# Attention in quarter steps with a written TensorE order, and experts gated sequence by sequence, in a two-layer kernel

## The chip, the core and the metric

The kernel runs on one core of a Trainium2 chip. It has five engines that run side by side and wait for each other through semaphores: TensorE (PE; its weight loads are shown as PEld), VectorE (DVE), ScalarE (ACT), GpSimd (POOL) and SyncE (SP), which here only starts transfers. The metric is the device time of one execution in microseconds. All data are float32.

## What is computed

Eight sequences of 256 tokens with 256 features pass four blocks, each added to its input after a layer norm:

```python
x = x + attn(layernorm(x))     # w = x @ W.T in 16 heads of 16; q, k, v = rms_norm(w) * g1, g2, g3
                               # att = q k^T / 4; score = softmax(att, -1) + softmax(att, -2)
                               # (score @ v) @ W
x = x + moe(layernorm(x))      # 4 experts, 2 for each token, silu(x w1) * (x w3) @ w2,
                               # and one shared expert for all tokens
x = x + rwkv(layernorm(x))     # time mixing: three recurrences along the tokens of a sequence
x = x + moe2(layernorm(x))     # 8 experts with biases, 2 for each token,
                               # g * sigmoid(1.702 g) * (l + 1) @ w2
```

Queries and keys come from the same w, so the att matrix of one head is symmetric. Exponentials computed once therefore serve both softmaxes, which have the same sums.

## The kernel before

The kernel writes its instructions as a Python program over tiles. A scheduler then puts each engine's instructions in an order of its own, by their place in the program and by estimated times, and adds the waits. Tiles come from pools; a pool holds so many buffers of each name, and a new tile waits until a buffer of that name is free. PSUM has three kinds of buffers here: `sc` for scores, `ps` for transposes, projections and values, `mm` for the experts' products.

The sequences are handled in two groups: five (`GROUPS[0]`) and three (`GROUPS[1]`). The experts of each block take their tokens group by group. A group passes these parts, methods of the class `Experts`: `front` (layer norm, transposes and gate for each sequence, then the choice of two experts and `route`, which works out a slot for each token), `sends` (POOL scatters tokens to DRAM, two transfers for each 128 tokens), `shared` (the expert for all tokens, or in the second layer the biases), `tiles` (128 sorted tokens at a time: fetch, transpose, up, transpose, down, write back) and `combine` (POOL gathers the results, DVE adds them). In `tiles` the stages of neighbouring tiles overlap: a step fetches tile j+3, transposes j+1, does up for j, transposes the hidden values of j-1 and does down for j-2. In the second layer the product that makes `h` stands on POOL (line 807).

Attention is `attention_bounded` (from line 404). For each sequence, `prepare` does the norm, transposes, projection (line 433) and the rms norm of all heads at once: squares on ACT, sums on DVE, the power -1/2 on POOL (line 442), and the product `n` on DVE (line 444). `turn` transposes `n` (line 453) and makes keys, queries and values. For each half of the heads (`u`) and each half of the tokens (`t`), `exponentials` does four score matmuls of 32 rows by 512 columns (line 477), their exponentials on ACT (lines 482 and 490), and sums, reciprocals and scaled values `nv` on DVE. `values` multiplies them (line 505), for one parity of heads at a time over both token halves; `project_heads` transposes the result, adds its two parts, transposes again and projects (line 536). The generator `steps` walks through this: while the exponentials of one half are made, the values of the half before are multiplied.

`layers` puts the parts together. `weave` takes several generators, each with a number, and advances the one that is behind its share, so their instructions stand in the program in turn; `take` cuts a generator. Group one's attention stands alone, with four `ps` and four `sc` buffers. Then come two `ps`, three `sc` and three `mm`, and the parts of the experts are woven with the attention of group two:

```python
weave((one.front(), 7), (take(attention, 3), 3))
weave((one.sends(), 10), (one.shared(), 5), (take(attention, 8), 8))
tiles = one.tiles()
weave((take(tiles, 12), 12), (attention, 16))
actx.close()
weave((two.front(), 5), (take(tiles, 3), 3))
weave((two.sends(), 6), (tiles, 10))
```

The second layer is built in the same way, with time mixing (`rwkv`, a generator of some eight steps for each sequence, of which two run at once) in attention's place: the first group's mixing is woven with the tiles of group two, and the second group's with the second layer's experts.

Of the kernel before, what the change touches and what calls it, by code (L numbers as in the profile page):

```python
# [13 lines left out]
AX = mybir.AxisListType  # L14

P = 128
B, T, D = 8, 256, 256
NTOK = B * T
NC = D // P
# [47 lines left out]
def two_layers(  # L67
# [336 lines left out]
    def attention_bounded(ap1, ap2, ep, fresh):  # L404
# [21 lines left out]
        def prepare(b):  # L426

            ps = fresh()[0]
            xt = turned(layer_norm(ap2, b, "xn"), ap2, "xnT", ps, nc.scalar)
            pw = ps([P, TT, D])  # L430
# [12 lines left out]
            n = ap2.tile([P, TT, NH, DH], F32, tag="n", name="n", bufs=3)  # L443
            nc.vector.tensor_tensor(n, pw4, rr.unsqueeze(3).to_broadcast([P, TT, NH, DH]), ALU.mult)
            seq[b] = dict(n=n)
# [55 lines left out]
        def values(b, u, es, par, py):  # L501

            for t in range(TT):
                for p in range(4):
                    nc.tensor.matmul(
                        py[STRIP * p : STRIP * (p + 1), par, :],
                        lhsT=seq[b]["nv"][:, t, 8 * u + 2 * p + par, :],
                        rhs=es[t, p][:, par, :],
                        start=(t == 0),
                        stop=(t == TT - 1),  # L510
                    )
            if par:
                nc.scalar.copy(seq[b]["yT"][:, u], py)

        def project_heads(b):
            ps = fresh()[0]
            q = seq.pop(b)
            y = ap2.tile([P, TT, NH, DH], F32, tag="y", name="y")
            for t in range(TT):
                pz = ps([P, 2, 4, 2, 2 * DH])  # L520
                for u in range(2):
                    for par in range(2):
                        nc.tensor.transpose(pz[:, u, :, par, :], q["yT"][:, u, par, ts(t, P)], ident)
                z = pz.rearrange("p u k a d -> p (u k a) d")
                nc.vector.tensor_tensor(
                    y[:, t],
                    z[:, :, DH:],
                    q["r"][:, t, :].unsqueeze(2).to_broadcast([P, NH, DH]),
                    ALU.mult,
                )  # L530
                nc.vector.tensor_tensor(y[:, t], y[:, t], z[:, :, 0:DH], ALU.add)
            yT = turned(y.rearrange("p t h d -> p t (h d)"), ap2, "yT2", ps, nc.scalar)
            po = ps([P, TT, D])
# [7 lines left out]
        def steps(seqs):  # L541

            prepare(seqs[0])
            yield
            turn(seqs[0])
            yield
            before = None
            for b, after in zip(seqs, seqs[1:] + (None,)):
                for u in range(2):
                    es = {}  # L550
                    py = fresh()[0]([P, 2, T]) if before else None
                    for t in range(TT):
                        exponentials(b, u, t, es)
                        if before:
                            values(*before, t, py)
                        yield
                    if before and before[1]:
                        project_heads(before[0])
                    yield
                    if after is not None:  # L560
                        (turn if u else prepare)(after)
                    yield
                    before = (b, u, es)
            py = fresh()[0]([P, 2, T])
            for par in range(2):
                values(*before, par, py)
            project_heads(before[0])
            yield

        return steps  # L570

# [22 lines left out]
    class Experts:  # L594
# [7 lines left out]
        def __init__(self, layer, k, weights, lnp, mp, rt, ps, mm):  # L602
# [5 lines left out]
            self.sent, self.back = (d[k][0 : P * self.n_tiles, :] for d in (sent, back))  # L608

        def front(self):  # L610

            rt, ps, nt, n = self.rt, self.ps, self.nt, self.n_experts
            self.xns, self.xts = [], []
            gw = (gw1, gw2)[self.layer]
            logit = rt.tile([P, nt, n], F32, tag="logit", name="logit")
            for i, b in enumerate(self.seqs):
                xn = layer_norm(self.lnp, b, "xm", bufs=max(len(g) for g in GROUPS))
                xt = turned(xn, self.mp, "xmT", ps, nc.scalar, bufs=2 if self.layer else max(len(g) for g in GROUPS))
                self.xns.append(xn)
                self.xts.append(xt)  # L620
                lg = ps([P, TT, n])
                for t in range(TT):
                    for c in range(NC):
                        nc.tensor.matmul(
                            lg[:, t, :], lhsT=xt[:, c, ts(t, P)], rhs=gw[:, c, :], start=(c == 0), stop=(c == NC - 1)
                        )
                to = logit[:, TT * i : TT * (i + 1), :]
                if self.layer:
                    nc.vector.tensor_tensor(to, lg, gb2.unsqueeze(1).to_broadcast([P, TT, n]), ALU.add)
                else:  # L630
                    nc.vector.tensor_copy(to, lg)
                yield
# [404 lines left out]
    def layers(is_bounded):  # L1037
# [4 lines left out]
        with ExitStack() as pctx, ExitStack() as ctx0, ExitStack() as actx:  # L1042
# [14 lines left out]
            if is_bounded:  # L1057
# [3 lines left out]
                with ExitStack() as p1:  # L1061
# [3 lines left out]
                    for _ in steps(GROUPS[0]):  # L1065
                        pass
# [121 lines left out]
```

## Time and profile before

| | us |
|---|---|
| median of three runs | 982.57 (981.32 to 987.0) |
| the profiled execution, as a run | 987.99 |
| its span, first to last instruction | 986.2 |
| attention of the first five: first score to last output projection | 34.3 to 209.7 |
| gates of those five; logits of the last | 210.4 to 235.9 |
| sends of the first group | 250.6 to 282.0 |
| tiles of the first group | 294.2 to 486.4 |
| sends of the first group in the second layer | 717.0 to 743.6 |
| last product of the tiles | 960.8 |

Times of stages are read from the trace, in microseconds from the first instruction. Several of the parts run at once; the table only gives their ends. A matmul in float32 leaves two records. The profile's granted clock is the share of full speed that TensorE's throttle allows; over the span it is 0.867. POOL's power of 128x32 (line 442) takes 5433 ns on average, eight times in all; each send and gather (lines 715 and 844) about 996 ns, 64 times each. A table load on ACT takes 1283 ns.

### The profile page before, as it was taken

The page shows a single profiled execution, that of the slowest core. Times are in us where ns is not written, and L with a number is a line of the kernel's source. Part 1 is how long each engine was busy: PE and PEld are TensorE (multiplying, and loading weights), DVE is VectorE, ACT ScalarE, POOL GpSimd, SP SyncE. Part 2 cuts the span into 40 slices and gives each one's busy share as a digit, 9 for nine tenths or more (in the row PEclk, how much of TensorE's full clock was granted, in tenths as well). Part 3 has the DMA queues.
Part 4 walks back from the last instruction along what each step waited for, and adds up shares of the span by engine and source line. Part 5 has one row for each costly group of instructions (what it writes and reads, how often), then busy time and mean ns, then how long its engine had stood idle before and what let it go on. Part 6 is the DMA issues. An engine that isn't in the chain of part 4 may idle for free. (4 is left out here: it accounts for less than half of the span.)

```text
span 986.2 us, 11005 instructions
## 1 busy us (share of the span) xinstructions
PE 786.5 (80%) x3248; PEld 466.8 (47%) x3248; DVE 497.8 (50%) x1173; ACT 362.2 (37%) x697; POOL 278.0 (28%) x357
## 2 busy tenths in 40 slices
PE   2787987988699899999969989855376988596890
PEld 1323423355455445665746665544243655353550
DVE  4453453524334333331256888887856784334432
ACT  1342442424347556542215525531213363222330
POOL 4313112002731100012171112234173232516424
PEclk9967767757899999999989999996657999799995
DMA  8820000000120001122130000014821211224413
GB/s 265 297 80 1 1 0 1 1 0 1 59 71 21 29 20 36 59 68 90 52 99 27 27 27 17 17 32 132 259 86 64 70 59 50 90 65 143 134 61 104
DMA packets 57763, 66.98 MB, mean 68 GB/s; under 512 B 7480, under 2 KB 51552, under 8 KB 57696
## 3 DMA queue, kind: packets, MB, share of 16 engines
q1 hardware_dynamic: 50016, 48.79, 15.4%
q0 software_dynamic: 6144, 16.79, 5.4%
q10 hardware_dynamic: 1536, 0.60, 0.2%
q8 instruction: 31, 0.51, 0.2%
q14 instruction: 36, 0.29, 0.1%
HBM read 38.61 MB, written 27.54 MB: 67 GB/s over the span
## 5 line engine op out<-in xcount | busy, mean ns | idle before, releaser
L477 PE MATMUL sc<-qT,kT 32*128 32x512 f32 x256 | 112.6, 791 | 4.3 <-ACT e L490 4.3
L176 POOL TENSOR_TENSOR rs<-mv,eps_ln 128x2 f32<-128x2 f32 x32 | 7.2, 228 | 329.5 <-DVE mv L174 279.8
L791 PE MATMUL mm<-v1s,xgT 128*128 x184 | 92.0, 623 | 0.0
L785 ACT COPY hT<-ps 128x256 f32<-128x256 f32 (+1 forms) x84 | 39.3, 468 | 136.7 <-PE ps L783 128.1
L715 POOL DMA_INDIRECT sent<-xm,slot x64 | 63.7, 996 | 83.3 <-DVE pick L690 65.3
L490 ACT ACTIVATE e<-sc,minus 128x512 f32<-128x512 f32 x96 | 62.4, 693 | 65.9 <-PE sc L477 43.6
L491 DVE TENSOR_REDUCE s<-e 128x2 f32<-128x512 f32 x96 | 62.6, 681 | 42.5 <-ACT e L490 42.0
L844 POOL DMA_INDIRECT y<-back,slot x64 | 63.7, 995 | 69.4 <-DMA back<-yg 41.6
L791 PE MATMUL mm<-w3s,xgT 128*128 x152 | 73.0, 597 | 3.1 <-DVE h L813 3.1
L791 PE MATMUL mm<-w1s,xgT 128*128 x152 | 74.3, 608 | 1.4 <-issue 1.4
L791 PE MATMUL mm<-w2s,hT 128*128 x304 | 72.2, 379 | 0.0
L783 PEld LDWEIGHTS ps<-ident,h 128*128 128x128 f32 x244 | 30.8, 143 | 66.7 <-issue 34.1
L807 POOL TENSOR_TENSOR h<-h,hb 128x256 f32<-128x256 f32 x46 | 34.7, 756 | 94.3 <-ACT h L806 94.2
L783 PE MATMUL ps<-ident,h 128*128 128x128 f32 x244 | 42.7, 281 | 21.4 <-POOL h L807 15.3
L791 PEld LDWEIGHTS mm<-w2s,hT 128*128 128x128 f32 x304 | 54.7, 190 | 6.3 <-issue 0.5
L818 DVE COPY yg<-mm 128x256 f32<-128x256 f32 x84 | 35.4, 421 | 44.0 <-PE mm L791 39.0
L813 DVE TENSOR_TENSOR h<-h,mm 128x512 f32<-128x512 f32 x38 | 25.9, 681 | 57.6 <-PE mm L791 44.9
L804 DVE TENSOR_TENSOR hb<-mm,b1rows 128x512 f32<-128x512 f32 x46 | 31.6, 687 | 43.6 <-PE mm L791 34.7
L442 POOL TENSOR_TENSOR rr<-rr,minus_half 128x32 f32<-128x32 f32 x8 | 43.5, 5433 | 31.5 <-DVE rr L441 31.5
L847 DVE SCALAR_TENSOR_TENSOR x<-y,share,x 128x256 f32<-128x256 f32 x64 | 31.6, 499 | 40.7 <-DMA y<-back,slot 39.5
L785 ACT COPY xgT<-ps 128x256 f32<-128x256 f32 x84 | 31.0, 370 | 57.5 <-PE ps L783 44.1
L791 PE MATMUL mm<-v2s,hT 128*128 x184 | 50.7, 400 | 0.8 <-ACT hT L785 0.8
(209 smaller groups left out, 1413.3 us busy)
## 6 DMA issues: line engine op xcount, KB each, us to landing
xg<-sent SPq DMA_DIRECT2D x84, 128.0 KB
back<-yg SPq DMA_DIRECT2D x84, 128.0 KB
sent<-zero SPq DMA_DIRECT2D x46, 128.0 KB
x<-in_x_dram SPq DMA_DIRECT2D x8, 256.0 KB
w1s<-in_w_dram SPq DMA_DIRECT2D x4, 512.0 KB
w3s<-in_w_dram SPq DMA_DIRECT2D x4, 512.0 KB
w2s<-in_w_dram SPq DMA_DIRECT2D x4, 512.0 KB
v1s<-in_v1g_dram SPq DMA_DIRECT2D x8, 256.0 KB
```

The costliest lines, as they stand in the source:

```text
L442: nc.gpsimd.tensor_tensor(rr, rr, minus_half.rearrange("p (t h) -> p t h", h=NH), ALU.pow)
L477: nc.tensor.matmul(pa, lhsT=q["kT"][rows, u, ts(t, P)], rhs=q["qT"][rows, u], start=True, stop=True)
L490: nc.scalar.activation(e, pa, AF.Exp, bias=minus)
L491: nc.vector.tensor_reduce(q["s"][:, t, h : h + 2], e, AX.X, ALU.add)
L715: inst = nc.gpsimd.indirect_dma_start(out=self.sent, out_offset=self.index(k, t), in_=self.xns[t // TT][:, t % TT, :], in_offset=None).ins
L783: nc.tensor.transpose(pt[:, c, :], src[:, ts(c, P)], ident)
L785: nc.scalar.copy(to, pt)
L791: nc.tensor.matmul(po.unsqueeze(1), lhsT=lhsT[:, c, :], rhs=w[:, ds(e, 1), c, :], start=(c == 0), stop=(c == n - 1))
L804: nc.vector.tensor_tensor(hb.unsqueeze(1), ph.unsqueeze(1), self.weights[2][:, ds(e_dve, 1), :], ALU.add)
L807: nc.gpsimd.tensor_tensor(s, s, hb[:, I2:], ALU.mult)
L818: nc.vector.tensor_copy(yg, py)
L844: nc.gpsimd.indirect_dma_start(out=y, out_offset=None, in_=self.back, in_offset=self.index(k, at))
```

## The change

Attention's stages become separate functions: `norm`, `project_in`, `turn`, `exponentials`, `values`, `to_tokens`, `turn_back`, `project_heads`. The new `steps` gives each of them a step number for each sequence, four steps to a sequence, and emits within a step in a fixed order of functions. `values` now does one token half and both parities, a step after its exponentials. The gate of layer one (`norm`, `flip`, `judge`) follows each sequence in the same steps. Around attention, `tc.manual_schedule(engines={ENG.PE})` keeps TensorE's instructions in the order in which the program has them; the other engines keep the scheduler's. `front` is cut: its part for one sequence is `norm`, `flip` and `judge`; the rest is `choose`. Time mixing calls a function at each sequence's end, which does the gate of layer two. Buffers change: `e` 10 to 9, `n` 3 to 2; in the stage of attention with experts `mm` 3 to 2 and `ps` 2 to 3. In the second layer, for its last group of experts (`self.last`), the product for `h` is on DVE.

```diff
-        def values(b, u, es, par, py):
+        def values(b, u, t, es):
-            for t in range(TT):
+            q = seq[b]
+            if t == 0:
+                q["py"] = fresh()[0]([P, 2, T])
+            for par in range(2):
                 for p in range(4):
...
-                        start=(t == 0),
-                        stop=(t == TT - 1),
+                        start=(t == 0 and par == 0),
+                        stop=(t == TT - 1 and par == 1),
                     )
-            if par:
-                nc.scalar.copy(seq[b]["yT"][:, u], py)
+            if t == TT - 1:
+                nc.scalar.copy(q["yT"][:, u], q["py"])
...
+        def steps(seqs, after):
+            late = {}
+            def at(n, f, *args):
+                late.setdefault(n, []).append((f, args))
+            for i, b in enumerate(seqs):
+                n = 4 * i + 4
+                at(max(n - 5, 0), norm, b)
+                at(max(n - 4, 0), project_in, b)
+                at(n - 2, turn, b)
                 for u in range(2):
                     es = {}
                     for t in range(TT):
+                        at(n + 2 * u + t, exponentials, b, u, t, es)
+                        at(n + 2 * u + t + 1, values, b, u, t, es)
+                    at(n + 2 * u + 3, to_tokens, b, u)
+                at(n + 6, turn_back, b)
+                at(n + 7, project_heads, b)
+                for k, f in enumerate(after):
+                    at(n + 7 + k, f, b)
+            order = (norm, turn, exponentials, project_in, to_tokens, values, turn_back, project_heads) + tuple(after)
+            for n in range(max(late) + 1):
+                for f, args in sorted(late.get(n, []), key=lambda x: order.index(x[0])):
+                    f(*args)
+                yield
...
-                    nc.gpsimd.tensor_tensor(s, s, hb[:, I2:], ALU.mult)
+                    (nc.vector if self.last else nc.gpsimd).tensor_tensor(s, s, hb[:, I2:], ALU.mult)
...
+                    with tc.manual_schedule(engines={ENG.PE}):
+                        for _ in steps(GROUPS[0], (one.norm, one.flip, one.judge)):
+                            pass
...
+                psum.update(pool=p2.enter_context(tc.tile_pool(name="p2", bufs=1, space=PSUM)), mm=2, ps=3, sc=3)
+                one.choose()
+                tiles = one.tiles()
+                if is_bounded:
+                    attention = steps(GROUPS[1], (two.norm, two.flip, two.judge))
+                    with tc.manual_schedule(engines={ENG.PE}):
+                        weave((one.sends(), 10), (take(attention, 6), 6), (one.shared(), 5))
+                        weave((take(tiles, 12), 12), (attention, 13))
+                    actx.close()
...
+            two.choose()
+            weave((two.sends(), 6), (tiles, 13))
...
-            weave((mixing(GROUPS[0]), 36), (tiles, 15))
+            weave((mixing(GROUPS[0], norm_of(three)), 36), (tiles, 15))
+            three.choose()
             weave((two.combine(), 3))
...
+            ahead = mixing(GROUPS[1], norm_of(four))
+            weave((three.sends(), 10), (three.shared(), 5), (take(ahead, 6), 6))
+            tiles = three.tiles()
+            weave((take(tiles, 17), 17), (ahead, 16))
+            four.choose()
+            weave((take(tiles, 3), 3))
+            weave((four.sends(), 6), (four.shared(), 3), (tiles, 9))
+            weave((three.combine(), 5), (four.tiles(), 21))
+            weave((four.combine(), 3))
```

`one` and `two` are the groups of layer one; `three` and `four` those of layer two, which were also called `one` and `two` before.

## The prediction

> **What bounds the kernel now.** I read four views in this order: the page's slices, the busy time by stage, the timeline of one sequence of the first attention stage, and the list of waits. The page says that no engine is full over the span, and that the TensorE clock is short in slices 2 to 11.
>
> ```profile
> PE 786.5 (80%) x3248; PEld 466.8 (47%) x3248; DVE 497.8 (50%) x1173; ACT 362.2 (37%) x697; POOL 278.0 (28%) x357
> PEclk9967767757899999999989999996657999799995
> ```
>
> The stages: five sequences of attention alone (34 to 210 us), attention of three sequences beside expert tiles (294 to 405), tiles (to 486), then time mixing beside tiles, the second layer's experts, and the last tiles.
>
> ```profile
> 115.50:153.00 37.50, 31.73 (x134) 13.15 (x133) 16.52 (x40) 14.46 (x34) 7.98 (x7) 0.73 0.00 1
> 352.00:405.60 53.60, 52.36 (x248) 27.67 (x242) 19.90 (x43) 35.89 (x60) 0.89 (x2) 1.00 0.10 30
> 580.00:650.00 70.00, 65.00 (x273) 44.13 (x272) 59.45 (x127) 33.91 (x51) 14.24 (x19) 1.00 0.06 21
> ```
>
> Columns: window, length, busy PE, PEld, DVE, ACT, POOL, then granted clock. In the attention stage one sequence takes 37.5 us while DVE works 16.5 and ACT 14.5; PE looks busy for 31.7 at a clock of 0.73. The two later stages are full of PE at the full clock. Of PE's 31.7 us the scores alone hold 16.7, and the timeline of the sequence before shows why.
>
> ```profile
> 115.50:153.00 37.50, 16.73 (x32) 4.36 (x32) 0.73 0.00 1
> ```
>
> (the same window, PE and PEld of the scores' line alone)
>
> ```profile
> 89.48 0.69 PE L453 MATMUL ps<-ident,n 128*128 128x128 f32 x2 [4.81 <-DVE n L444]
> 90.09 2.07 PE L477 MATMUL sc<-qT,kT 32*128 32x512 f32 x2
> 92.20 0.69 ACT L490 ACTIVATE e<-sc,minus 128x512 f32<-128x512 f32 x1 [5.19 <-PE sc L477]
> 92.50 2.07 PE L477 MATMUL sc<-qT,kT 32*128 32x512 f32 x2
> ...
> 99.28 1.14 PE L477 MATMUL sc<-qT,kT 32*128 32x512 f32 x8
> ```
>
> A score is two records. Alone between transposes it takes 2.07 us; four in a row take 1.14 us together at 99.28. And PE stood still for 4.8 us for `n`, whose cause is POOL's power:
>
> ```profile
> DVE n L444 <- POOL rr L442: 48.5, 8, 11.2
> ACT e L490 <- PE sc L477: 43.6, 25, 5.2
> DVE s L491 <- ACT e L490: 42.0, 33, 3.2
> PE ps L783 <- POOL h L807: 15.3, 9, 4.8
> ```
>
> The first line is 5.43 us of POOL per sequence with PE, ACT and DVE starving behind it. The last is another place: expert tiles of layer 2 waiting for a product on POOL behind its gathers.
>
> **What the skill says.** "TensorE: Matmul & The Clock Gate", section "HAM oscillation — how this bites in real kernels": an idle gap of over about 3.4 us drops PE to half rate. The trace agrees: one 4.8 us gap per sequence, clock 0.73. The same page, "The mechanism" of its part 3: matmuls in different 32-row groups overlap; here 1.14 us for four against 1.12 us for one at the full clock (78.57). The same page, "Step-by-step: what each phase is for": only weight loads are pulled ahead, matmuls stay in order (the trace of before doesn't show what that costs: there a scheduler made PE's order). So an order that is written down also stalls as written. "ScalarE: Activation LUTs", "What ACT_TABLE_LOAD costs": a measured 1283 ns, the very mean of the rows here; exp beside Silu pays it twice per exchange.
>
> **The change, part by part.** Sums are against the profiled execution (span 986.2 us, run 988.0), which lies 5.4 above the median 982.57; I subtract the saving from the median.
>
> *Attention of the first five.* Each sequence becomes four steps, with every stage of its neighbours at a fixed step. Work per sequence, from start-to-start times in the timeline and row means:
> - ACT: 12 exponentials at 0.62, 8 half ones at 0.45, seven copies and squares at 0.59 (the experts' one included): 7.5 + 3.6 + 4.1 = 15.2 us.
> - DVE: 12 sums at 0.62, four reciprocals with `nv` at 0.49, qT 1.4, n 0.7, rr 0.9, y 2.0, x 0.7, two layer norms at 1.83, logits 0.2: 19.0 us.
> - PE at full clock: scores 4 x 1.12, two projections at 1.99, values 4 x 1.07, six sets of transposes at 0.6, gate 1.05: 17.4 us.
>
> The power stays: from the projection's end to `turn` the trace has 7.9 us (119.0 to 126.9). `turn` now stands two steps on, ahead of that step's scores. PE has 5.5 us of other work before it (values 1.07, experts' transposes 0.6, scores 1.12, tokens 0.6, values 1.07, gate 1.05), so 2.4 us stay open; queues on ACT (up to 2.8 us of exponentials ahead of the square) and DVE add some 2. A stall of about 4 us per sequence again starves the clock; I take 0.8. Period: 17.4 / 0.8 + 4 = 25.8, say 26 us. Lower bound: DVE's 19.0 + 2 = 21. Upper: PE at the old clock, 17.4 / 0.73 + 8 = 32.
>
> Start: scores at 31 us in place of 34.3, as one projection less stands before them. End of 20 steps: 31 + 5 x 26 = 161. The last sequence then runs out: values, yT, transposes, y, transposes, copy, projection, x about 9 us; norm, transposes, gate 8: logits at 178. Before: 235.9 (the logit copy at 235.75). **Saved 58 us**; of it about 40 from the attention and 18 from gating that no longer follows for all five.
>
> *Choice to first tile.* The chain of small DVE operations to the route's matmul took 10.6 us before, and 5 more to the first send (250.6). The 20 sends are 1.27 apart: 25 us. POOL now has two powers among them, before one (260.7): 11 us in place of 5.5; the sends behind them wait. 178 + 15.5 + 36 + 3 = 233 for the first tile, 55 us against 58 before (235.9 to 294.2). PE has 37 us for that time (shared expert 5 x 5.6, six steps 8.7), so it is covered if PE isn't held. **Saved 3**, bounds -8 and +15.
>
> *Tiles beside attention.* PE owes 23 tiles at 5.8 us (six forms: 0.4 + 1.88 + 1.88 + 0.6 + 1.89, less overlap) = 133, and 3 x 17.4 - 8.7 = 43.5 of attention: 177 us. The order can't adapt, `mm` has two banks in place of three, and exponentials share ACT with Silu at two table loads (2.6 us) per exchange: ACT has about 8 us per 10 us pair. I take 6% of stall: 187 against 192 (294.2 to 486.4). **Saved 5**, bounds -10 and +15. The second choice starts without the norms of its three sequences; tiles cover it, as they did.
>
> *Time mixing and layer 2's gate.* Norm, transposes and gate of each sequence move into the mixing stage: 5 x 1.65 us of PE and 5 x 2 of DVE where PE is 93% and DVE 85% busy: 5 us lost. After the last mixing only one sequence's norm and gate remain, 8 us, where 19 passed (x at 682.6, last logit at 701.7): 11 gained. The weight loads (issued 681.8 to 700) stay ahead of the first tile at 752. Net 6. In the second group 3 us net: no fronts amid tiles (823 to 838), but four mixing steps more beside 17 tiles, where DVE is 80% busy.
>
> *Product on DVE.* For the last 18-odd tiles h is made on DVE (0.4 us, as the 128x256 addition of line 531, up to 0.7 as line 813 at twice the size) and not on POOL (0.756) behind gathers at 0.96 each. PE gaps at 896.7, 907.9, 914.2 and 920.2 are 4.8, 2.6, 3.1 and 1.2: 11.7. DVE also holds the combine's additions, which wait for gathers, so part returns: 8 saved, bounds 0 and 11. Smaller buffers (`e` 9, `n` 2) cost nothing: eight `e` live at once, and `n` of the sequence before the last is dead by then.
>
> Sum: 58 + 3 + 5 + 6 + 3 + 8 = 83. Forecast 982.6 - 83 = 899.6, **900 us**.
>
> **Rivals.**
> 1. *As worked out*, 900, its own range 875 to 925: 0.55.
> 2. *The pipeline runs at DVE's pace*: 21 us per sequence saves 25 more, and a warm PE lets tiles and attention go at 100%, 10 more: 865. For it: no engine holds more than 19 us. Against: the power's 7.9 us in front of `turn`. 0.20.
> 3. *The written order stalls*: 32 us per sequence gives back 30, stalls of 14% in the weave with tiles give back 14: 944. For it: in 294 to 405 a free order held PE at 0.97 to 1.00, and the banks shrink. 0.17.
> 4. *Slower*: one mechanism, the step as a serial chain. If a step's scores wait for the step before to release the banks, and values for exponentials, sums and `nv` of the step just done, a step at half clock is 2.1 + 2.8 + 1.2 + 2.1 + handovers, some 10 us and not 6.5. It decides from where 36 steps (20 + 16) cost 83 us more, at 6.5 + 83/36 = 8.8 us each. At 10: +126 - 83, 1026 us. Against it: values lie one step behind their exponentials. 0.06.
> 5. *No difference*, gains eaten in the weave: 983: 0.02.
>
> **How the numbers follow.** The likeliest gives 900. From 855 to 950 the range holds rival 2, most of rival 3 and the bounds of the first; rival 4 and the far ends are left out. Half a per cent, some 5 us, is what a measurement can tell from nothing. Faster 0.92, same 0.02, slower 0.06.
>
> **What would show it.** Periods of `turn` at about 26 us in the first stage; scores in runs of eight records of 1.1 us; PE's wait for `n` at 2 to 5 us each; granted clock 0.8; logits of the fifth sequence near 178; first tile near 233; last tile of the first group near 420; no PE gap over 2 us behind h in the last tiles. Wrong, if a step costs over 8.8 us, if the sends start later than 205, or if PE stands in front of the first tile for over 15 us with attention written behind it.

## The result and the profile after

The changed kernel takes 978.06 us (median of 20 runs, 976.69 to 982.82); the kernel before took 983.21 beside it (20 runs). The ratio is 0.9948, with an interval of 0.9932 to 0.9965: 5 us saved where 83 were forecast. The profiled execution took 982.58 us with a span of 980.8.

First, the page of the changed kernel, busy time and granted clock.

```profile
PE 748.6 (76%) x3248; PEld 460.7 (47%) x3248; DVE 501.1 (51%) x1208; ACT 356.0 (36%) x693; POOL 261.7 (27%) x338
PEclk9998895897889997999799779965678798799995
```

The clock is better in most of slices 3 to 9, with attention alone, and worse later: slices 23 and 24, in the first mixing, read 7 where they read 9 before. So something was gained early and lost late. Marks on the time axis show how much. Each is the start or end of one named piece of work, the same in both traces; the mark of a mixing is the start of its output projection. The forecast column adds up the prediction's own terms.

| mark | before | after | lead | lead forecast |
|---|---|---|---|---|
| last logit of the first five (their experts can be chosen) | 235.8 | 159.4 | 76 | 58 |
| first tile | 294.2 | 227.3 | 67 | 61 |
| tiles of the first group done | 486.4 | 449.3 | 37 | 66 |
| first group's last mixing, output projection | 679.4 | 665.0 | 14 | 61 |
| its route in layer two | 711.9 | 680.3 | 32 | 72 |
| second group's last mixing, output projection | 826.1 | 822.0 | 4 | 72 |
| its route | 841.2 | 834.3 | 7 | 75 |
| end | 986.2 | 980.8 | 5 | 83 |

The lead rises to 76 and is given back in two places of some 30 us, the tiles beside attention and the mixing. The next view is the busy time by stage, the columns as in the prediction (window, length, busy PE, PEld, DVE, ACT, POOL, granted clock, DMA share, GB/s). Of the kernel before, the stages not yet shown:

```profile
294.20:405.00 110.80, 105.28 (x471) 55.51 (x469) 41.44 (x87) 70.80 (x121) 7.98 (x7) 0.98 0.09 27
405.00:486.40 81.40, 79.38 (x357) 50.84 (x356) 23.11 (x89) 25.30 (x44) 12.54 (x14) 1.00 0.22 70
486.40:679.40 193.00, 154.05 (x621) 105.48 (x619) 146.71 (x297) 73.46 (x113) 61.79 (x69) 0.93 0.13 40
679.40:752.00 72.60, 40.81 (x163) 30.00 (x163) 47.48 (x125) 15.12 (x28) 30.50 (x32) 0.64 0.50 162
752.00:826.10 74.10, 67.63 (x269) 42.72 (x268) 56.71 (x103) 33.37 (x71) 22.12 (x31) 0.97 0.19 61
```

Of the changed kernel: one period of the first attention, the tiles in four windows, the first group's mixing, and layer two up to the second group's last mixing.

```profile
66.80:90.10 23.30, 18.84 (x145) 10.13 (x145) 16.27 (x43) 14.39 (x35) 7.95 (x7) 0.87 0.00 1
227.30:280.00 52.70, 46.37 (x194) 22.14 (x191) 17.23 (x38) 29.35 (x54) 6.17 (x3) 0.81 0.05 16
280.00:335.00 55.00, 50.33 (x255) 26.83 (x254) 21.80 (x50) 36.57 (x65) 0.89 (x2) 0.94 0.07 22
335.00:390.00 55.00, 49.26 (x210) 30.02 (x209) 20.34 (x87) 19.75 (x34) 2.84 (x5) 0.88 0.14 46
390.00:449.30 59.30, 59.30 (x232) 38.00 (x231) 11.54 (x21) 14.94 (x29) 10.56 (x11) 1.00 0.21 68
449.30:665.00 215.70, 167.52 (x663) 114.83 (x661) 148.31 (x309) 76.29 (x117) 61.39 (x70) 0.88 0.12 36
665.00:717.70 52.70, 28.50 (x91) 18.78 (x92) 27.61 (x87) 8.77 (x18) 26.44 (x29) 0.56 0.67 224
717.70:822.00 104.30, 85.81 (x317) 53.95 (x317) 75.13 (x132) 43.05 (x82) 25.71 (x34) 0.88 0.14 43
```

What to see: a sequence takes 23.3 us where it took 37.5 (the two sequences ahead of it, while the pipeline fills, 17.6 and 20.5). The tile stage before held PE at 0.98 to 1.00; now its first three windows read 0.81 to 0.94. The first mixing grew from 193.0 to 215.7 us, its clock fell from 0.93 to 0.88, with 42 matmul records more: four of the group's five gates stand in it. In layer two the first tile comes 20 us sooner after the mixing (52.7 for 72.6), but the time from there to the second group's last mixing grew by 30 (104.3 for 74.1).

The pipeline itself, in the timeline of one step (start, length, engine, operation; in brackets the idle time before and its releaser):

```profile
83.84 5.43 POOL L445 TENSOR_TENSOR rr<-rr,minus_half 128x32 f32<-128x32 f32 x1 [3.48 <-DVE rr L444]
...
89.30 0.69 DVE L447 TENSOR_TENSOR n<-ps,rr 128x512 f32<-128x512 f32 x1 [5.54 <-POOL rr L445]
...
90.05 1.12 PE L456 MATMUL ps<-ident,n 128*128 128x128 f32 x4 [4.42 <-DVE n L447]
...
91.10 2.09 PE L480 MATMUL sc<-qT,kT 32*128 32x512 f32 x8
```

PE still waits for `n` once per sequence, here 4.4 us, 18.5 us in four waits (17.9 in four before). The scores now come four together, all eight records in one run: 2.09 us here at half clock, right after that gap, as long as one score alone took there before. Later in the sequence, at 100.57, such a run takes 1.14 us.

The waits in the first group's mixing show what lengthened it (engine, what it waited for, us in total, times, longest):

```profile
PE ps L191 <- DVE xm L181: 18.4, 4, 9.5
```

No such row stood there before. `xm` is the normed input of a gate. The longest of these four, in the timeline of the changed kernel:

```profile
641.87 0.15 DVE L175 BATCH_NORM_AGGREGATE mv<-st 128x2 f32<-128x6 f32 x1
...
644.37 0.95 POOL L865 DMA_INDIRECT y<-back,slot  x1 [0.30 <-issue]
645.34 0.20 POOL L177 TENSOR_TENSOR rs<-mv,eps_ln 128x2 f32<-128x2 f32 x1
645.70 0.96 POOL L865 DMA_INDIRECT y<-back,slot  x1 [0.16 <-issue]
646.68 0.73 POOL L178 TENSOR_TENSOR rs<-rs,minus_half 128x2 f32<-128x2 f32 x1
647.45 0.74 DVE L181 TENSOR_SCALAR xm<-x,mv,rs 128x256 f32<-128x256 f32 x2 [3.63 <-POOL rs L178]
647.92 1.22 PE L191 MATMUL ps<-ident,xm 128*128 128x128 f32 x4 [9.49 <-DVE xm L181]
...
649.81 1.88 PE L644 MATMUL ps<-gw,xmT 128*128 128x8 f32 x8 [0.67 <-ACT xmT L197]
```

The variance is known at 642.0, but the norm's two small operations stand in POOL's queue between the combine's gathers and end at 647.4. DVE stands still 3.6 us for them with the mixing's own work behind, PE stands 9.5, and its transposes and gate then run at half clock (1.22 and 1.88 us, at full clock 0.60 and 1.03). The other waits are of 5.1, 2.6 and 1.2 us. No gathers stand in front of those norms, and POOL had been idle for over 10 us: there PE had only come in its order to the transposes before statistics, power and `xm` were through.

The row of 18.4 us isn't what the stage lost, for other waits shrank. In the kernel before, one wait in this stage was

```profile
PE ps L947 <- DVE dx L874: 11.3, 1, 11.3
```

and it is 2.7 us in the changed kernel. From the windows above, PE's idle time in the first mixing grew by 9 us (39.0 to 48.2) and its busy time by 13.5 (154.05 to 167.52), in part more work and in part the same work at a lower clock.

### The profile page after: what moved, and what is told of

It reads as the page before. It is cut to its first block, busy times and chain, and to the rows that moved or that the text cites. A ratio compares the mean times of both kernels' runs of the same rounds, so it can differ in the third digit from the quotient of the medians.

```text
span 980.8 us, 11031 instructions
## 1 busy us (share of the span) xinstructions
PE 748.6 (76%) x3248; PEld 460.7 (47%) x3248; DVE 501.1 (51%) x1208; ACT 356.0 (36%) x693; POOL 261.7 (27%) x338
## 3 DMA queue, kind: packets, MB, share of 16 engines
q1 hardware_dynamic: 50016, 48.79, 15.4%
## 5 line engine op out<-in xcount | busy, mean ns | idle before, releaser
L812 PE MATMUL mm<-v1s,xgT 128*128 x184 | 97.8, 654 | 0.8 <-ACT xgT L806 0.7
L812 PE MATMUL mm<-w1s,xgT 128*128 x152 | 78.9, 642 | 1.1 <-issue 0.3
L480 PE MATMUL sc<-qT,kT 32*128 32x512 f32 x256 | 62.9, 741 | 15.0 <-ACT e L493 13.1
L494 DVE TENSOR_REDUCE s<-e 128x2 f32<-128x512 f32 x96 | 60.2, 678 | 25.6 <-ACT e L493 25.3
L493 ACT ACTIVATE e<-sc,minus 128x512 f32<-128x512 f32 x96 | 59.2, 694 | 37.1 <-PE sc L480 37.1
L445 POOL TENSOR_TENSOR rr<-rr,minus_half 128x32 f32<-128x32 f32 x8 | 43.5, 5437 | 76.2 <-DVE rr L444 76.2
L806 ACT COPY xgT<-ps 128x256 f32<-128x256 f32 x84 | 30.9, 370 | 74.1 <-PE ps L804 73.6
L812 PEld LDWEIGHTS mm<-w3s,xgT 128*128 128x128 f32 x152 | 29.2, 195 | 42.4 <-issue 34.2
```

Of the source, the lines that this page charges most:

```text
L445: nc.gpsimd.tensor_tensor(rr, rr, minus_half.rearrange("p (t h) -> p t h", h=NH), ALU.pow)
L480: nc.tensor.matmul(pa, lhsT=q["kT"][rows, u, ts(t, P)], rhs=q["qT"][rows, u], start=True, stop=True)
L493: nc.scalar.activation(e, pa, AF.Exp, bias=minus)
L494: nc.vector.tensor_reduce(q["s"][:, t, h : h + 2], e, AX.X, ALU.add)
L806: nc.scalar.copy(to, pt)
L812: nc.tensor.matmul(po.unsqueeze(1), lhsT=lhsT[:, c, :], rhs=w[:, ds(e, 1), c, :], start=(c == 0), stop=(c == n - 1))
```

## The experiments

The theory after the traces: early choice in layer two gains nothing, because that layer is paced by a chain from the first group's last mixing to the second group's last mixing, which takes some 147 us however early the first group's experts are chosen; the gates inside the mixing therefore only cost. Rivals for the lost lead: the written order in the stage of attention with tiles, the smaller PSUM shares there, and the exchange of tables on ACT. The runs came in three sets, each beside the kernel before on one chip. The chips differ, so times are compared by ratio, and stages within a set where that can be done. "Chain" stands for the time from the first group's last mixing to the second group's.

### First set: the change's parts alone

**Gates behind the mixing.** The changed kernel with layer two as before; the first layer and the product on DVE stay.

```diff
-            weave((mixing(GROUPS[0], norm_of(three)), 36), (tiles, 15))
-            three.choose()
+            weave((mixing(GROUPS[0]), 36), (tiles, 15))
...
-            ahead = mixing(GROUPS[1], norm_of(four))
+            ahead = mixing(GROUPS[1])
+            weave((three.front(), 7), (take(ahead, 4), 4))
```

> The changed kernel with the second layer's gates put back behind the mixing (fronts of five and of three, as before the change); attention, first layer and the product on DVE stay changed. Theory A (the first layer's lead of 37 us at the end of its tiles is real, and gating sequence by sequence inside the time mixing spends it): about 945 us, 0.96 of before, and the lead at the end of the first layer's mixing is still 30 us or more. Rival B (the second layer ends where it ends because of something that the gates don't touch, so the lead is lost in any case): within 5 us of the changed kernel, 973 to 983.

957.32 us, ratio 0.9683 (0.9637 to 0.9728). The windows of this run, first mixing and the chain after it:

```profile
455.70:648.50 192.80, 153.94 (x621) 105.45 (x619) 146.90 (x297) 73.42 (x113) 61.57 (x69) 0.93 0.13 40
648.50:795.20 146.70, 108.49 (x430) 72.89 (x430) 104.30 (x228) 48.40 (x99) 52.53 (x63) 0.81 0.35 111
```

The first mixing is back at 192.8 us (193.0 before) and the chain at 146.7, what it was before. The first group's route comes 17 us later after the mixing (32.4 for 15.3), and nothing is lost by it. At the end of the first mixing the lead is the 31 us that theory A gave; in time the run stays 12 us behind that theory's 945.

**Gates alone.** The kernel before with the new layer two only (the gates inside the mixing, the last product on DVE, and `e` and `n` with fewer buffers). The edit against the kernel before, cut to its core:

```diff
-            weave((mixing(GROUPS[0]), 36), (tiles, 15))
+            weave((mixing(GROUPS[0], norm_of(three)), 36), (tiles, 15))
+            three.choose()
...
-            ahead = mixing(GROUPS[1])
-            weave((one.front(), 7), (take(ahead, 4), 4))
...
+            ahead = mixing(GROUPS[1], norm_of(four))
```

> The kernel before with the second layer's part of the change alone: gates inside the mixing, the last product on DVE (and e with 9, n with 2 buffers, for room). Theory A: it loses what the changed kernel loses after its tiles, some 30 us: 1005 to 1020, 1.02 to 1.04 of before. Rival B: within 6 us of before, 977 to 989, as the gates neither cost nor give.

1027.99 us, ratio 1.0381 (1.0311 to 1.0451). First mixing 214.3 us, chain 159.4. This part of the change taken by itself makes the kernel slower by 39 us, of which 34 stand in these two stretches.

**Four score banks.** In the stage of attention with tiles `sc` gets four buffers and `ps` two.

```diff
-mm=2, ps=3, sc=3)
+mm=2, ps=2, sc=4)
```

> The changed kernel with four sc and two ps buffers in the stage of attention with experts, in place of three and three. Theory C (with three banks the fourth score of each step waits on PE for the table load and the first exponential, 1.6 to 2.4 us, and then runs alone for 1.1 to 2.1): the stage from the first tile to the last of the first group falls from 222 us by 20 to 35. What is left at the end depends on theory A: 965 to 975 if the mixing spends part of it. Rival D (two ps buffers stall transposes by as much): the stage within 8 us of 222, the time 972 to 985.

1007.27 us, ratio 1.0164 (1.0111 to 1.0218). The tile stage took 234.2 us against 220.7 in the two neighbours on this chip. Waits of PE in that stage:

```profile
PE ps L804 <- ACT byT L520: 7.5, 4, 2.4
PE ps L804 <- issue: 5.0, 2, 3.3
PE ps L551 <- DVE y L540: 4.0, 2, 2.0
```

The wait of the scores for exponentials is gone from the list (11.5 us before this edit), and waits for `ps` that are larger in sum stand in its place: the tiles' transposes now wait for attention's buffers. The stage is longer than either theory allowed.

**Product on POOL.** Only the last group's product goes back.

```diff
-(nc.vector if self.last else nc.gpsimd).tensor_tensor(s, s, hb[:, I2:], ALU.mult)
+nc.gpsimd.tensor_tensor(s, s, hb[:, I2:], ALU.mult)
```

> The changed kernel with the product h of the last tiles on POOL again. Prediction's step: 8 us back, 986. Rival: DVE's additions of the gathered rows hold it up as much as POOL's gathers did, since gaps of 3.1, 1.1, 2.1, 1.4 and 3.5 us stand in front of those transposes in the changed kernel too: within 3 us of 978.

997.01 us (20 runs), ratio 1.0074 (1.0051 to 1.0097). The whole difference isn't the product's: the first tile came at 236.8 us, 9.5 later than in the changed kernel, before any such product runs. From the second route to the end it takes 148.5 us against 146.5 and 145.9 in the two traces of the changed kernel, so the product could be worth 2 to 3 us. But these are traces of other chips. On this run's own chip the kernel with four score banks has the product on DVE and takes 148.7: no gain at all. With the gates behind the mixing the kernel before takes 145.0 there with the product on POOL, and the four such traces below and above take 142.1 to 143.3 with it on DVE. So the product is worth 0 to 3 us. Why it is no more, the waits of PE there say, first with the product on POOL, then the changed kernel:

```profile
PE ps L804 <- POOL h L828: 12.4, 8, 4.3
```

```profile
PE ps L804 <- DVE h L828: 11.1, 5, 3.4
PE ps L804 <- POOL h L828: 3.6, 4, 2.0
```

Much of the wait moved with the product to DVE's queue. The late first tile is another matter; this run's timeline shows where it begins:

```profile
203.57 0.69 DVE L780 TENSOR_TENSOR hs<-hs,mm 128x512 f32<-128x512 f32 x1 [6.21 <-remote]
```

The changed kernel has 3.27 us there, ended by PE. "Remote" is a releaser that the profile can't name. Five other runs with the written order have the same stall (6.3 to 6.5 us) and their first tile at 233 to 237; the two traces of the changed kernel have neither, with the first tile at 227.3 and 227.5. All six with the stall are of the chips of the first two sets, and no trace of the third set's chip has one; the kernel before has such a stall too, 5.7 us at 283.5. Among the runs with the written order it goes with the chip or the hour. Its cause stays open, and runs of different sets that differ by under 10 us are compared by stages here.

### Second set: are the costs to be avoided?

**Gates late.** The norm stays at the end of a mixing; transposes and gate follow four mixing steps later.

```diff
+                    for d in list(due):
+                        d[1] += 1
+                        if d[1] > 4:
+                            due.remove(d)
+                            later(d[0])
```

> The changed kernel, but a sequence's gate in the second layer is split: its norm at the end of its mixing as in the change, its transposes and gate matmuls four mixing steps later. Theory A1 (the loss is PE standing in order before transposes whose norm isn't ready: gaps of 2.6 and 5.1 us and a halved clock after each): the first group's mixing falls from 216 us (216.1 with the product on POOL, 193 with gates behind) to about 198, the early choice keeps its 15 us, and the second group's stage from 104 to about 85: 940 to 960, 0.95 to 0.97 of before. Rival A2 (the added DVE and ACT work of five gates costs it, wherever it stands): within 8 us of the changed kernel, 0.987 to 1.003.

974.91 us, ratio 0.9865 (0.9811 to 0.992). The two windows, first mixing and chain:

```profile
458.00:658.00 200.00, 160.19 (x664) 111.16 (x662) 147.44 (x308) 75.82 (x117) 61.47 (x70) 0.91 0.13 39
658.00:810.40 152.40, 113.22 (x407) 71.88 (x407) 104.30 (x220) 51.70 (x100) 52.17 (x63) 0.78 0.33 107
```

First mixing 200.0 us (215.7), chain 152.4 (157.0). PE's wait for `xm` is gone from its list, and with it two thirds of the first mixing's loss: of the 15.7 us PE's idle time gives 8.4 and its busy time 7.3, with as many matmul records, at a clock of 0.91 in place of 0.88. Some 7 us are left for the work itself. So theory A1 has the first mixing right. It doesn't have the second group: the chain is still 6 longer than with no gates in it, and the time as a whole is at the edge of the rival's range.

**Ten ahead.** Four more of the second group's mixing steps stand beside the sends.

```diff
-            weave((three.sends(), 10), (three.shared(), 5), (take(ahead, 6), 6))
+            weave((three.sends(), 10), (three.shared(), 5), (take(ahead, 10), 10))
...
-            weave((take(tiles, 17), 17), (ahead, 16))
+            weave((take(tiles, 17), 17), (ahead, 12))
```

> The changed kernel with ten steps of the second group's mixing woven with the sends and twelve with the tiles, in place of six and sixteen. If the second group's stage (first tile to last mixing, 104 us, before the change 74) is long because its mixing starts late: it falls by 15 us or more, 0.975 to 0.985 of before. If it is long because of the gates within it: under 5 us, 0.99 to 1.00.

998.28 us (20 runs), ratio 1.005 (1.0024 to 1.0076). The first tile came 58 us after the first group's route where it came 37 after, and the stretch from there to the last mixing shrank from 104 to 84. The chain stayed at 157.0: what is moved ahead of the tiles is paid ahead of the tiles. Neither reading foresaw that.

**Tanh for Silu.** In the first layer's experts `tanh` stands where Silu is; the run leaves Silu out, and its outputs are other numbers.

```diff
-                    nc.scalar.activation(s, pu, AF.Silu)
+                    nc.scalar.activation(s, pu, AF.Tanh)
```

> The changed kernel with tanh in place of Silu in the first layer's experts (shared and routed), which leaves the exact Silu out: the same ACT time, without an exchange of tables between exponentials and Silu if tanh shares the exponentials' table. Theory C (the fourth score waits for the table load, 1.28 us, and the first exponential): the stage from first tile to last of the first group falls from 221 us by 12 to 25, 0.97 to 0.985 of before. Rival (the three banks alone do it): under 6 us.

983.53 us, ratio 0.9932 (0.9902 to 0.9962), with a tile stage of 206.8 us against 221.9 and 221.2 in the two runs above on this chip. The groups of the changed kernel have these rows, and the run with tanh has no load on either line:

```profile
L832 ACT ACT_TABLE_LOAD x18 | 23.1, 1283 | 3.5 <-PE mm L812 3.2
L493 ACT ACT_TABLE_LOAD x11 | 14.1, 1283 | 2.4 <-PE sc L480 2.2
```

That agrees with the Trainium skill, "ScalarE: Activation LUTs", section "Table sets: the hidden batching unit", which has exp and tanh in one set; these 29 loads, gone with tanh, say that Silu is in another. The exchange costs ACT 37 us, and within the stage ACT's busy time falls from 100.4 us (gates late, same chip) to 73.3 and the stage by 15. The whole time doesn't show it: the ratio is where the changed kernel's is. The first tile came 8 us later than in the changed kernel (235.4), behind the stall of this chip, and the first mixing and the part after the second route each took 3 us more. What the exchange is worth at the end is not shown.

**The scheduler in the weave.** The written order is taken from the stage of attention with tiles alone.

```diff
-                    with tc.manual_schedule(engines={ENG.PE}):
-                        weave((one.sends(), 10), (take(attention, 6), 6), (one.shared(), 5))
-                        weave((take(tiles, 12), 12), (attention, 13))
+                    weave((one.sends(), 10), (take(attention, 6), 6), (one.shared(), 5))
+                    weave((take(tiles, 12), 12), (attention, 13))
```

> The changed kernel without the written TensorE order in the second stage (attention of the last three beside sends, shared expert and tiles); the first five keep it. Theory C (order and three banks make each attention step 2 to 3 us dearer on PE): the first tile comes earlier than 227 or the stage of tiles takes less than 215: 0.97 to 0.99 of before. Rival (without the order scores stand alone between transposes again, as before the change, 2.1 us for each of a step's parts): no gain or slower, 0.99 to 1.01.

972.53 us, ratio 0.9813 (0.9768 to 0.9858). The tiles in this run:

```profile
220.60:430.30 209.70, 196.14 (x886) 112.02 (x883) 71.16 (x197) 100.75 (x182) 20.50 (x21) 0.97 0.13 41
```

The clock is 0.97 again, the stage takes 209.7 us (221.9 and 221.2 with the order on this chip), and the first tile comes 60 us after the choice, not 68. In the third set, where no trace has a "remote" stall, it comes after 54 to 56 us without the order, and after 69 with it. Part of the gap in front of the first tile was PE standing in its order for the shared expert's `hs`, in the waits of the changed kernel from the choice to the first tile:

```profile
PE mm L783 <- DVE hs L780: 15.8, 5, 8.2
```

In the run without order this row is 5.8 us. In the changed kernel, at the longest of these waits (8.2 us, to 183.0), `hs` stood on DVE behind `n`, and `n` behind a power of 5.46 us that POOL began at 176.19, among the sends.

### Third set: both undone, and how far

**The changed kernel again**, the same program.

> The changed kernel as it is, beside the others on one chip: 0.995 of before, as measured. If e4's 1.007 was the product alone, this stays at 0.995; if that chip and hour cost the order of the first weave some microseconds (stalls of ACT and DVE released by 'remote' that e4 and e1 show and the first trace of the changed kernel doesn't), this reads 1.000 to 1.005 and the product is worth the 3 us that the stages show.

978.02 us, ratio 0.9936 (0.9918 to 0.9953); first tile 227.5, mixing 214.2, chain 156.8. It is on the chip of the three below. As this chip shows no "remote" stall, the run can't tell how much of the 1.007 with the product on POOL was the stall.

**Two parts undone.** Gates behind the mixing and no written order in the weave, both edits as above.

> The changed kernel with both costly parts undone: gates of the second layer behind the mixing as before, and the scheduler's TensorE order in the weave of attention with experts; the first five sequences keep the written order, all steps stay. If the two costs are separate (26 us and 18 to 27 us): 0.94 to 0.955 of before. If one hides the other: 0.96 to 0.97, as with the gates alone.

916.30 us, ratio 0.9312 (0.9278 to 0.9346): 68 us faster than before and the best of all. The windows of this run, tiles, first mixing, up to the first tile of layer two, second mixing, rest:

```profile
214.50:421.90 207.40, 195.73 (x887) 111.59 (x884) 71.25 (x197) 100.93 (x182) 20.45 (x21) 0.97 0.13 42
421.90:612.30 190.40, 152.68 (x620) 104.58 (x618) 146.93 (x297) 73.53 (x113) 61.87 (x69) 0.93 0.14 41
612.30:682.00 69.70, 39.72 (x162) 29.47 (x162) 47.20 (x129) 15.17 (x28) 30.61 (x34) 0.65 0.52 169
682.00:756.30 74.30, 67.42 (x271) 42.65 (x269) 55.24 (x101) 33.25 (x71) 21.34 (x30) 0.97 0.19 60
756.30:913.30 157.00, 108.02 (x410) 64.25 (x410) 64.14 (x163) 37.11 (x94) 49.59 (x55) 0.86 0.31 96
```

Of 62 us against the changed kernel beside it, 25 are gone when the tiles end (446.8 to 421.9), and 37 between there and the second group's last mixing (23.8 in the first mixing, 12.8 in the chain). Neither cost hides the other. By whole times they more than add: against the changed kernel's 0.9948 the run with gates behind gained 26 us and the run with the scheduler's order 13, together 39, and both at once give 62, which is also more than the forecast had. Both single runs carry a "remote" stall before their first tile (6.4 us on DVE, 3.1 on ACT) that this one doesn't; by stages they gained 33 (mixing and chain) and 20 (from the choice to the last tile), together 53. The rest isn't explained.

**First gates late.** The same, with the first group's gates put back into its mixing, in the late form.

```diff
+            weave((mixing(GROUPS[0], *norm_of(three)), 36), (tiles, 15))
+            three.choose()
```

> As e10, with the first group's gates of the second layer inside the mixing again, but their transposes and matmuls four steps behind their norm (e5's way), and the second group's behind as before. In e5 the first group's end of tiles to its route took 215 us, in e1 225; in e1 the second group 129 us, in e5 149. So 5 to 10 us under e10: 0.93 to 0.945. If the mixing of the second group, four steps later against its tiles, takes that back: equal to e10 within 3 us.

926.96 us, ratio 0.9421 (0.9385 to 0.9456): 10.7 us slower than with the gates behind, where a gain was expected. The windows, first mixing and chain:

```profile
419.60:617.00 197.40, 158.11 (x664) 110.25 (x662) 147.56 (x308) 75.87 (x117) 61.63 (x70) 0.93 0.13 39
617.00:765.10 148.10, 109.65 (x388) 69.57 (x388) 100.95 (x218) 50.92 (x99) 52.13 (x63) 0.78 0.34 110
```

The first group's route came 12 us earlier (632.4 for 644.7), the first tile of layer two as well (669.8 for 682.0), and the second group's last mixing still came 9 later. The gates' work costs the first mixing 7.0 us, and the chain doesn't shrink in return.

**No written order.** The best version with the order taken from the first attention too.

```diff
-                    with tc.manual_schedule(engines={ENG.PE}):
-                        for _ in steps(GROUPS[0], (one.norm, one.flip, one.judge)):
-                            pass
+                    for _ in steps(GROUPS[0], (one.norm, one.flip, one.judge)):
+                        pass
```

> As e10, without the written order in the first stage too, so that no TensorE order is written anywhere; the quarter steps stay. If the written order makes the first stage's gain: periods of turn go from 23.3 us back towards 30 to 37 and the time is 30 to 70 us over e10. If the steps themselves make it: periods within 2 us of 23.3 and the time within 8 us of e10.

920.89 us, ratio 0.9348 (0.9309 to 0.9387), 4.6 over the best. The periods of `turn` are 18.2, 20.8, 23.3 and 23.5 us without any order; with it, in the best version, they are 17.3, 20.7, 23.3 and 23.5. The scores stand in runs of eight records all the same. The quarter steps make the early gain; the order adds at most 5 us to the whole, 2 of them up to the last logit of the first five (162.2 for 160.3).

## Why the prediction was wrong

By its own steps: what each term was to add to the lead, and what it added in the traces. Route three and route four are those of the first and the second group in layer two.

| step | forecast, us | measured, us |
|---|---|---|
| attention of the first five, up to the choice | +58 | +76 |
| choice to first tile | +3 | -10 |
| tiles beside attention | +5 | -30 |
| first mixing with its gates, up to route three | +6 | -5 |
| second group's mixing and gates, up to route four | +3 | -25 |
| product on DVE, route four to the end | +8 | -1.5 |

The miss of 78 us stands in two places. The tiles beside attention, with the way to their first tile, were to add 8 and took 39. The gates inside the mixing were to add 9 and took 30. A surplus of 18 in attention, from a price set too high, hides a part of it, and the product on DVE misses by 9 more.

**Attention alone: the mechanism right, the price too high.** The form was as worked out: one stall of some 4.4 us per sequence and PE's work for the rest. The work takes 18.8 us at a clock of 0.87, not 21.8 at 0.8, so the period is 23.3 and not 26; the first two periods are shorter still (17.6 and 20.5). The last gates also come faster than a period, as the pipeline runs empty (logits at 132.7, 146.9, 159.4). In this stage the rival that runs at DVE's pace was nearer, with a lead of 83.

**Choice to first tile: outside its bound.** The prediction counted what stands behind two powers on POOL, the sends, and called PE covered "if PE isn't held". It was: `hs` stood behind `n`, `n` behind the power, PE in its order behind `hs`, 15.8 us in place of the 9.5 before. The loss of 9.5 lies past the bound of 8, and the prediction's own sign of being wrong, PE standing over 15 us in front of the first tile, came true. Without the order its 55 us come out: 54 to 56 in the third set. The first tile is near its forecast (227.3 for 233) only because two errors cancel.

**Tiles beside attention: the sum was too small from the start.** It gave PE 177 us of work. The kernel before had 184.7 busy in that stage (105.28 + 79.38), with 828 matmul records; the new stage has 887, for more of the second group's attention stands in it (80 records of scores for 56, 176 of values for 144). The run with the scheduler's order needs 196 us of PE in 209.7. On top the written order costs 12 us (222.0 against 209.7), where all stall together was put at 6%, 10 us. So of the 35 us between forecast and measurement the order makes 12 and the sum 23. The five figures that the prediction has for a tile add up to 6.65 us; it took 5.8, "less overlap", and without that guess its sum would be the 196 that the run has (23 x 6.65 + 43.5). The busy time of the same stage before was the better source.

**Gates inside the mixing: here the mechanism failed.** The prediction costed "5 x 1.65 us of PE", lost 5 us by it, and gained 11 for the shorter tail. The trace has 22.7 us lost in the first mixing, with four of the five gates in it. The gates' work was sized nearly right (7 us in the late form). What was priced at nothing is that PE stands in its order for `xm`, and that it runs at half clock after such a gap: the other 15.7 us, gone when the transposes come four steps later. In the longest of the waits the norm's small POOL operations had queued behind the gathers of `combine`, of which the prediction doesn't speak. Then it didn't ask what the earlier route would bring forward: the route does come 17 us sooner after the mixing, more than the 11 forecast, and the second group's last mixing doesn't come sooner for it. From the first group's last mixing to the second group's:

| kernel | first mixing | route after it | chain |
|---|---|---|---|
| before | 193.0 | 32.5 | 146.7 |
| gates behind | 192.8 | 32.4 | 146.7 |
| two parts undone | 190.4 | 32.4 | 144.0 |
| first gates late | 197.4 | 15.4 | 148.1 |
| gates late, both groups | 200.0 | 15.4 | 152.4 |
| changed | 215.7 | 15.3 | 157.0 |
| ten ahead | 219.0 | 15.1 | 157.0 |

The chain follows the gates inside it, never the route. With the gates in place it is 154.5 to 161.5 us in the six traces that aren't in this table, so single microseconds in it mean nothing. Which resource makes its 147 us wasn't isolated; only that neither an early route nor more steps ahead shortens it. Nor was it isolated why gates lengthen it.

**Product on DVE: too large.** 0 to 3 us of the 8. The prediction saw that DVE also holds the combine's additions and let them take 4; most of the gain went there. Three gaps of 2.1 to 3.4 us behind `h` stand in the last tiles, where none over 2 was to be.

The rival of the stalling written order (944) had the weave with tiles right, 14 us where the order itself cost 12. It didn't price the way to the first tile, where the order cost another 15 us (68.8 with it, 54.2 without, third set), and put its larger part, 30, in the first attention, which ran faster than forecast. The rival that ends at no difference has the number, 983, and half of the reason. It spoke of gains eaten in the weave: from the choice to the last tile 39 us went, the other 32 in the mixing and after it, for which there was no rival at all. That the two parts undone give 916, inside the forecast range, is in part luck: there too attention gains more than was forecast and the tiles lose where they were to gain.

The stall behind `n` is still there, and the Trainium skill's account ("TensorE: Matmul & The Clock Gate", section "HAM oscillation — how this bites in real kernels") holds in that the 4.4 us gap is followed by half clock. In the mixing a shorter one does it too: after 2.61 us before the transposes at 541.5 two records of `w1s` take 1.91 us at 547.3, which took 1.02 at 530.5. In the kernel before, eight records of `sc` behind a gap of 2.52 us take 3.64 us at 572.7, and in the changed kernel, behind 1.89 us, 1.99 at 535.2. The page gives some 3.4 us for the gap; here 2.5 was enough.

## What to carry to other kernels

Work moved off a tail into a full stage is priced by what stands behind it in the order of each engine, and not by its own duration alone: here four gates of 1.65 us cost 23. Before paying for an earlier event, follow the path from it to the end and ask whether anything starts sooner; here a stage bound from one mixing to the next took no profit from an early choice. Undo the parts of a bundle one by one: two losses of 25 and 37 us hid a gain of 68.

## What the runs showed of the hardware

Four row-tiled scores in a run of eight records take 1.14 us at full clock and 2.09 at half, where one alone takes 1.12 and 2.07 (kernel before), so they overlap in both states. ACT's table load is 1.28 us, and the exponential behind one started 1.30 us after the load did (233.02 to 234.32 in the changed kernel): nothing is seen there beyond the load itself. Before the first tile DVE stood for 6.2 to 6.5 us in six runs of the written order on two chips, with a releaser that the trace calls "remote", about when POOL's sends end. The changed kernel itself, with the same text up to there, has no such stall in two traces. What it is stays open.
